# A two-layer kernel: how its first batch is prepared, and when GpSimd does its odd jobs

## The chip, the cores and the metric

The kernel runs on one core of a Trainium2 chip. The metric is device time in microseconds (us) of one execution. TensorE is called PE here, VectorE DVE, ScalarE ACT, GpSimd POOL, and SyncE, which issues most of the DMAs, SP. Everything is float32. A difference of 0.2% (8.3 us) is about what can be told from no change at all.

## The reference, cut to what matters

The input x is 4 batches of 2048 rows of 256. Two layers are computed; each adds an attention-like part and a second part, both fed by the layer norm of its input.

```python
xn = layernorm(x)
r = sigmoid(xn @ Wa + ba);  i = sigmoid(xn @ Wx + bx)          # gates
at = sigmoid(Lam) * exp(-r * log 8);  bt = sqrt(1 - at*at) * (i * xn)
y = scan over time: y_t = at_t * y_{t-1} + bt_t                 # recurrence
# 4 of 16 heads per batch, chosen by top_k(softmax(mean_t(xn @ Wr + br)))
x = x + y + attention(xn, the 4 chosen heads) @ Wo + bo         # layer 0
xn = layernorm(x)
a = causal attention(xn, 16 heads of 16) @ W_o + b_o            # layer 1
xr, xk = mixes of xn with xn one row earlier (mu_r, mu_k)
x = x + a + sigmoid(xr @ W_r.T) * (relu(xk @ W_k.T)**2 @ W_v.T)
```

## The kernel before

The program is unrolled over the batches. Inside `in_order` the compute engines (PE, ACT, DVE, POOL) keep the order in which the code is written; SP is free of that, and so is the setup ahead of it, whose instructions are placed among the others when the program is built. Several streams of work are Python generators, advanced a step at a time by `steps`, so that their instructions interleave.

**Setup.** `load_x(0)` is called once for `x_next`, which nothing reads, and again in `prepared(0, ...)`: eight loads of 512 KB on SP. ACT issues the weights `wa`, `wx`, then the bias vectors into `rows` and `rowb` (15 small loads, L181 and L186), `wr`, `wo2`, and layer 1's weights. PE turns `rows` and `rowb` into columns (L189, L190), DVE copies them to `cols` (L191), and ACT makes `a_c` of them (L201, L202). The biases of the gates come from `cols` too. Then layer 1's value bias goes through `wo1` into `bo1_b` (L219 to L223), and `W_r`, `W_k`, `W_v` are turned (L231, L232).

**Norm of the first batch.** `go` in `prepared`: statistics of 16 tiles of 128 rows (L261, L262), one inverse root for all on POOL (L267), then for each of four blocks of 512 rows four normalised tiles (L274) and two turns into `xT` (PE L280, DVE L281). All of it runs ahead of the recurrence in batch 0; in later batches it runs under layer 1 of the batch before.

**Recurrence and choice.** `recurrence` computes 16 gate units (PE L296, four instructions each; ACT L298), then `chain` for each half of the channels: Exp, Square and Sqrt on ACT, products (L306, L314) and two scans (L318) on DVE. `choose` sums `xT` (L351), picks the heads (L359 to L379), loads their weights (L391 to L393) and scales them (L423 to L425). After the 16 steps come `added` (L432), queries (L462), keys (L479) and half of the values (`values0`, L448; its copies out of the banks, L450, alternate between ACT and DVE). Each of these ten steps also advances the recurrence by one.

**Attention 0.** `attention0` works on pairs of row tiles. It names its PSUM banks by hand: scores of the first tile go to banks 0, 5, 4, 7 and of the second to 2, 1, 3, 6. `lend(...)` makes the next users of `own_bank` take the banks named. In the first pair, values borrow banks 1 and 3, later 4 and 7.

**Layer 1.** Four groups `g` of four heads; in each, four blocks `q` of 512 rows; in each, `4q + 4` units `t`. A group has 40 units. `Weights.scores` makes transposed scores (L828), exponentials (L830), and for the last four units of a block a mask on POOL (L833). `weigh`, one unit behind, multiplies by the values (L839); ACT copies the product out (L845) and POOL adds it up (L846). `Leading` runs the row maxima (L803, L806, L809) 20 units ahead, and SP writes them into row 16 of each head's strip in the query tile (L873). POOL also does these jobs: for `0 < g < 3` it clears the next group's two strips (`heads.open`, L741) in units 0 and 2 of block 1, and `heads.copy` (L747) sends eight copies through SP from unit 3; in odd groups it multiplies a block by its inverse sums (L922) 12 slots after the block ended, two slots per unit (`spread` comes by DMA L918 and is shuffled on DVE, L921); and in group 1 it adds `bo1_b` to one tile of x in each of the first 16 units (L958).

Of the kernel before, what the change touches and what calls it, by code (L numbers as in the profile page):

```python
# [10 lines left out]
FP = mybir.dt.float32  # L11
# [7 lines left out]
P = 128  # L19
# [57 lines left out]
def two_layers(ctx: ExitStack, tc: tile.TileContext, x, Wa, Wx, ba, bx, Lam,  # L77
# [61 lines left out]
        n0 = n % (NT // 2)  # L139
        return both[n // (NT // 2)][:, n0:n0 + count, :]  # L140

    x_next = load_x(0)


    ident = const.tile([P, P], FP, tag="ident", name="ident")
# [26 lines left out]
        ACT.dma_start(t, v.partition_broadcast(P))  # L172
        return t

    wa, wx = load_w(Wa, "wa"), load_w(Wx, "wx")


    rows = c4.tile([18, P], FP, tag="c4", name="rows")
    POOL.memset(rows, 0.0)
    for i, v in enumerate((ba, bx, Lam, mu_r, mu_k, bo, bv1, bq1, bk1)):  # L180
        ACT.dma_start(rows[2 * i:2 * i + 2, :], v.rearrange("(c p) -> c p", p=P))  # L181

    rowb = c4.tile([3 * NH, P], FP, tag="c4", name="rowb")
    for i, v in enumerate((bq, bk, bv)):
# [26 lines left out]
    for i in range(2):  # L211
        ACT.dma_start(wo2[i * DH:(i + 1) * DH, :, :], Wo.rearrange("(k d) e -> d k e", d=DH))

    wq1, wk1 = load_w(Wq1, "wq1"), load_w(Wk1, "wk1")
    wv1 = load_w(Wv1, "wv1")
    wo1, bo1_b = load_w(Wo1, "wo1"), load_row(bo1, "bo1_b")

    bv_b = c4.tile([P, 2, P], FP, tag="c4", name="bv_b")
    DVE.tensor_copy(bv_b, bv1_c.unsqueeze(2).to_broadcast([P, 2, P]))  # L219
    ps = bank()  # L220
    for c in range(2):
        PE.matmul(ps[:, 0:D], lhsT=bv_b[:, c, :], rhs=wo1[:, c, :], start=(c == 0), stop=(c == 1))
    DVE.tensor_tensor(bo1_b, ps[:, 0:D], bo1_b, ALU.add)  # L223

    def transposed(w, name):
        n = load_w(w, name + "_n", c4, "c4")
        t = const.tile([P, 2, D], FP, tag=name, name=name)
        ps = bank().rearrange("p (c d) -> p c d", c=2)
        for c in range(2):
            for d in range(2):  # L230
                PE.transpose(ps[:, c, d * P:(d + 1) * P], n[:, d, c * P:(c + 1) * P], ident)  # L231
        DVE.tensor_copy(t, ps)  # L232
        return t

    w_rT, w_kT, w_vT = transposed(W_r, "w_rT"), transposed(W_k, "w_kT"), transposed(W_v, "w_vT")

    DVE.tensor_scalar(w_vT, w_vT, 0.5, None, ALU.mult)


    nms = []  # L240
# [200 lines left out]
    def values0(b, xT, wv_, v, banks_of):  # L441

        for n in range(NT // 2):
            ps = banks_of[0]()
            for i in range(2):
                t = 2 * n + i
                for c in range(2):
                    PE.matmul(ps[:, i * D:(i + 1) * D], lhsT=xT[c][:, t * P:(t + 1) * P], rhs=wv_[:, c, :],  # L448
                              start=(c == 0), stop=(c == 1))
            (DVE.tensor_copy if n % 2 else ACT.copy)(rows_of(v, 2 * n, 2), ps.rearrange("p (n d) -> p n d", d=D))  # L450
            yield

    def queries0(b, k, xT, ch, bank):
# [120 lines left out]
    def attention0(b, xT, xt, ch, recurring, first, v, rest_of_values, norm, opening, leading):  # L574
# [20 lines left out]
        for n in range(NA * NP):  # L595
# [38 lines left out]
            if before:  # L634
                for j, i, to in ((0, 0, 1), (0, 1, 3), (1, 0, 6)):
                    late.turn(j, i, *of(to))
                    late.keep(j, i, ACT.copy)
            else:
                lend(1, 3)
                steps(rest_of_values, 2)  # L640
                lend()
            for j, i in ((0, 0), (1, 1), (1, 0), (0, 1)):
# [241 lines left out]
    def layer1(b, heads, vs, opening, x1, prepare, leading):  # L884
# [15 lines left out]
        def divide(g, q, o):  # L900


            i, blk = g % 2, slice(q * QB, (q + 1) * QB)
            part = vals[g // 2][:, blk]

            if i == 0:
                sums[q] = sm.tile([P, QB // 16], FP, tag=f"sums1_{q}", name=f"sums1_{b}_{g}_{q}", bufs=1)
            few = sums[q]
            SP.dma_start(few[64 * i:64 * i + 64, :], o[DH1:P:32, :].rearrange("h (a r) -> h a r", a=16))
            for h in range(4):  # L910
                row = (4 * i + h) * DH1
                SP.dma_start(part[row:row + DH1, :], o[32 * h:32 * h + DH1, :])
            if i == 0:
                return

            def invert():
                DVE.reciprocal(few, few)
                SP.dma_start(spread[0:P:16, :].rearrange("h (a r) -> h a r", a=16), few)  # L918

            def multiply():  # L920
                DVE.stream_shuffle(spread, spread, [0] * 16 + [16] * 16)  # L921
                POOL.tensor_tensor(part, part, spread, ALU.mult)  # L922
                if g == NG - 1:
                    mixing.append(mix.block(q))
            later.put(8, invert)
            later.put(12, multiply)

        def weigh(before):
            g, q, unit = before
# [6 lines left out]
            steps(opening, 1)  # L936
        before = None
        for n, (g, q, w) in enumerate(attending()):
            if q == 1 and 0 < g < NG - 1:
                if w.t in (0, 2):  # L940
                    heads.open(g + 1, w.t // 2)
                elif w.t == 3:
                    heads.copy(g + 1, slice(0, T))
            m = leading.next()
            for h in range(0, 4, 2):
                w.scores(h)
                w.scores(h + 1)
                if m is not None:
                    m.scores(2 - h)
                    m.scores(3 - h)  # L950
            if before is not None:
                weigh(before)
            later.slot()
            later.slot()
            before = (g, q, w)
            if g == 1 and n % 40 < NT:
                xs = rows_of(x1, n % 40, 1)[:, 0, :]
                POOL.tensor_tensor(xs, xs, bo1_b, ALU.add)  # L958
            if g == NG - 1 and q == 2:
                steps(mix.ahead, 1)  # L960

            for _ in range(2 if m is None else 0):
                if mixing and not steps(mixing[0], 1):
                    mixing.pop(0)
            if g == NG - 1:
                if q == 0 and w.first:
                    norming, choosing = prepare()
                elif m is None:
                    steps(norming, 2)
# [75 lines left out]

    def prepared(b, ready):

        xt = load_x(b)
        norm = Norm(xt, f"0_{b}", own_bank)
        ch = Chosen()  # L1050
        ready.append((xt, norm.xT, ch))

        def go():
            for t in range(0, NT, 2):
                norm.stats(t)
                norm.stats(t + 1)
                yield
            norm.inverse(0, NT)
            yield
            for q in range(NQ):  # L1060
                norm.rows(q, 0, 2)
                yield
                norm.rows(q, 2, 4)
                yield
                yield
                for c in range(2):
                    norm.turn(q, c, DVE.tensor_copy)
                    yield
        return go(), choose(b, norm.xT, ch)

    NOTHING = iter(()), iter(())

    with in_order(tc):
# [2 lines left out]
        mixing = iter(())  # L1076
        for b in range(B):
            xt, xT, ch = ready.pop()
            steps(norming, 100)
            recurring = recurrence(b, xT, xt, ch)  # L1080
            for _ in range(16):
                steps(recurring, 1)
                steps(mixing, 2)
                steps(choosing, 1)
            steps(mixing, 100)
            steps(choosing, 100)
            v = [half_tile(f"v0_{b}_{i}").rearrange("p (n f) -> p n f", f=NA * DH) for i in range(2)]
# [4 lines left out]
            for stream, count in ((querying, 4), (keying, 2), (valuing, 4)):  # L1092
                for _ in range(count):
                    steps(stream, 1)
                    steps(recurring, 1)

            banks_of[0] = bank
            x1, norm = xt, Norm(xt, f"1_{b}", bank)
# [37 lines left out]
```

## Time and profile before

| | us |
|---|---|
| median of 3 runs (lowest to highest) | 4131.89 (4131.09 to 4131.98) |
| the profiled execution's own time | 4131.89 |
| its span | 4130.2 |
| PE busy | 4059.9 (98%) |
| DVE busy | 2937.5 (71%) |
| ACT busy | 2892.1 (70%) |
| POOL busy | 1058.9 (26%) |

The span is what the trace covers; 1.7 us of the execution lie around it. PE's share is so high that the time is almost the sum of its work and its stops, so the table of who waited for whom on PE is the list of what can be had without less work on PE. A page's busy share counts modelled matmul ends, and cannot show a PE at half its clock; the granted clock does.

### The profile page before, as it was taken

Reading aid. Unit: us, or ns where it says so; the run is one execution under the profiler, and the core shown is the slowest. Engines: PE = TensorE matmul, PEld = TensorE weight load, DVE = VectorE, ACT = ScalarE, POOL = GpSimd, SP = SyncE. Lnnn points to the kernel's source line nnn. Section 1 sums busy time; section 2 is a strip of 40 time slices with the busy share of each in tenths; the row PEclk is TensorE's granted clock in tenths of the full one; section 3 lists DMA queues with packets and bytes.
Section 4 is the critical chain, followed back from the end, with each engine's and each line's share of the span. In section 5 each row is a group of like instructions: output and inputs, shape, how many; then the busy total and the mean of one; then the engine's idle time right before and its main releaser. Section 6 shows DMA issues by size and latency. Waiting matters only on the chain.

```text
span 4130.2 us, 86165 instructions
## 1 busy us (share of the span) xinstructions
PE 4059.9 (98%) x32994; PEld 2275.4 (55%) x32994; DVE 2937.5 (71%) x7036; ACT 2892.1 (70%) x6593; POOL 1058.9 (26%) x1334
## 2 busy tenths in 40 slices
PE   6999999999999999999999999999999999999998
PEld 3777743335577774333457776433446777643334
DVE  5656778887566668888656566888856656688882
ACT  3777658886677766888667775688756777578874
POOL 0000016544100002654410000365450000036544
PEclk9999999999999999999999999999999999999999
DMA  3000011100100001110010000101000000101000
GB/s 89 1 12 2 7 19 18 37 7 17 28 2 12 1 9 17 18 38 7 18 25 1 12 1 12 16 16 38 7 19 24 1 12 1 22 6 18 18 6 24
DMA packets 70816, 65.77 MB, mean 16 GB/s; under 512 B 37234, under 2 KB 58628, under 8 KB 68868
## 3 DMA queue, kind: packets, MB, share of 16 engines
q1 hardware_dynamic: 66624, 57.19, 6.5%
q8 instruction: 260, 4.26, 0.4%
q10 hardware_dynamic: 3780, 3.07, 0.3%
q14 instruction: 152, 1.25, 0.1%
HBM read 16.70 MB, written 8.39 MB: 6 GB/s over the span
## 4 chain that ended last, share of the span: by engine, by line
PE 94%; DVE 3%; ACT 1%; POOL 1%; DMA 1%; issue 0%; ACTq 0%; SPq 0%; POOLq 0%; DVEq 0%
PE bank L828 15%; PE bank L803 13%; PE bank L839 13%; PE bank L521 11%; PE bank L546 11%; PE bank L500 11%; PE bank L1024 4%; PE bank L730 3%; PE bank L296 3%; PE bank L559 2%; PE bank L762 1%; PE bank L462 1%; PE bank L1012 1%; PE bank L479 1%; DVE mx L809 1%; PE bank L280 1%
## 5 line engine op out<-in xcount | busy, mean ns | idle before, releaser
L830 ACT ACTIVATE p<-bank 128x512 f32<-128x512 f32 (+3 forms) x2560 | 1175.2, 539 | 291.3 <-PE bank L828 156.2
L803 PE MATMUL bank<-k,q 32*128 32x512 f32 (+3 forms) x5120 | 1138.5, 566 | 4.4 <-DVE mx L809 1.3
L809 DVE TENSOR_REDUCE mx<-bank 128x1 f32<-128x512 f32 x1536 | 953.1, 683 | 216.2 <-PE bank L803 216.0
L828 PE MATMUL bank<-q,k 32*128 32x512 f32 (+3 forms) x5120 | 1091.6, 556 | 0.0
L846 POOL TENSOR_TENSOR o<-o,w 128x512 f32<-128x512 f32 (+3 forms) x576 | 628.0, 1090 | 760.0 <-ACT w L845 748.3
L515 ACT ACTIVATE p<-bank,nm 128x512 f32<-128x512 f32 x1024 | 696.6, 700 | 58.5 <-DVE nm L508 58.1
L828 PEld LDWEIGHTS bank<-q,k 32*128 32x128 f32 x5120 | 420.7, 184 | 532.8 <-ACT p L830 446.7
L504 DVE TENSOR_REDUCE mx<-bank 128x1 f32<-128x512 f32 x1024 | 635.4, 683 | 86.6 <-PE bank L500 86.6
L527 ACT COPY pT<-bank 128x512 f32<-128x512 f32 x768 | 404.7, 598 | 306.4 <-PE bank L521 303.9
L839 PE MATMUL bank<-p,v 128*17 128x512 f32 (+3 forms) x5120 | 602.7, 534 | 16.4 <-POOL p L833 11.5
L521 PEld LDWEIGHTS bank<-ident,p 128*128 128x128 f32 x4096 | 446.1, 141 | 143.3 <-issue 116.6
L806 DVE CUSTOM_DVE_ANT_0 bank<-bank,cmask 128x512 f32<-128x512 f32 (+3 forms) x1024 | 473.4, 521 | 70.8 <-PE bank L803 51.0
L521 PE MATMUL bank<-ident,p 128*128 128x128 f32 x4096 | 508.5, 276 | 0.0
L803 PEld LDWEIGHTS bank<-k,q 32*128 32x128 f32 x5120 | 430.2, 183 | 133.7 <-DVE mx L809 36.6
L267 POOL TENSOR_TENSOR rs<-rs,minus_half 128x4 f32<-128x4 f32 (+1 forms) x20 | 27.9, 1395 | 1852.1 <-DVE rs L266 1828.1
L546 PEld LDWEIGHTS bank<-pT,v 128*64 128x64 f32 x8192 | 444.5, 137 | 95.3 <-ACT p L515 94.0
L500 PE MATMUL bank<-k,q 64*128 64x512 f32 x2048 | 496.4, 603 | 0.0
L546 PE MATMUL bank<-pT,v 128*64 128x128 f32 x8192 | 475.4, 274 | 0.0
L845 ACT COPY w<-bank 128x512 f32<-128x512 f32 (+3 forms) x576 | 304.4, 529 | 101.5 <-PE bank L839 76.0
L527 DVE COPY pT<-bank 128x512 f32<-128x512 f32 x256 | 164.8, 685 | 293.1 <-PE bank L521 291.8
L839 PEld LDWEIGHTS bank<-p,v 128*17 128x17 f32 x5120 | 89.7, 95 | 431.5 <-ACT p L830 236.4
L833 POOL TENSOR_SCALAR_AFFINE_SELECT p<-p 128x256 f32<-128x256 f32 x512 | 206.8, 416 | 313.4 <-ACT p L830 306.8
(164 smaller groups left out, 3323.1 us busy)
## 6 DMA issues: line engine op xcount, KB each, us to landing
x<-in_L_attn_x_dram SPq DMA_DIRECT2D x20, 512.0 KB
q<-q SPq DMA_DIRECT2D x64, 128.0 KB
vals<-o SPq DMA_DIRECT2D x256, 32.0 KB
out_dram<-x SPq DMA_DIRECT2D x32, 256.0 KB
q<-qp SPq DMA_DIRECT2D x48, 128.0 KB
k<-kp SPq DMA_DIRECT2D x48, 128.0 KB
q<-nmT SPq DMA_DIRECT2D x256, 2.0 KB
q<-qp SPq DMA_DIRECT2D x64, 32.0 KB
```

The lines of the kernel that those rows point to most:

```text
L500: PE.matmul(self.s[j][i], lhsT=self.qT[i][half_, self.t * P:(self.t + 1) * P], rhs=self.kT[half_, j * QB:(j + 1) * QB], start=True, stop=True)
L504: DVE.tensor_reduce(self.mx[:, n:n + 1], self.s[j][i], AX.X, ALU.max)
L515: ACT.activation(self.p[j][:, i, :], self.s[j][i], AF.Exp, bias=self.nm, accum_out=self.sums[:, n:n + 1])
L521: PE.transpose(to[:, n * P:(n + 1) * P], self.p[j][:, i, n * P:(n + 1) * P], ident)
L527: copy(self.pT[:, n0:n0 + 4, :], self.tr[j, i].rearrange("p (n q) -> p n q", q=P))
L546: PE.matmul(acc[i * DH:(i + 1) * DH, 0:P], lhsT=self.v[h][:, n, self.k * DH:(self.k + 1) * DH], rhs=tile_.pT[:, 8 * h + n, :], start=(n == ...
L803: PE.matmul(s[:, 0:n], lhsT=self.qT[strip(h), self.qs], rhs=self.kT[strip(h), self.ks], start=True, stop=True)
L809: DVE.tensor_reduce(self.mx[:, h, :], s[:, 0:n], AX.X, ALU.max)
L828: PE.matmul(s[:, c0:QB], lhsT=self.kT[strip(h), self.ks], rhs=self.qT[strip(h), self.q0 + c0:self.q0 + QB], start=True, stop=True)
L830: ACT.activation(p[:, h % 2, c0:QB], s[:, c0:QB], AF.Exp, scale=SC1)
L839: PE.matmul(acc[32 * h:32 * h + DH1 + 1, c0:QB], lhsT=self.v[h], rhs=self.p[h // 2][:, h % 2, c0:QB], start=True, stop=True)
L846: POOL.tensor_tensor(self.o[:, c0:QB], self.o[:, c0:QB], w[:, c0:QB], ALU.add)
```

## The change

- x of batch 0 is loaded once: `x_first`, which `prepared` uses.
- The vectors stand ahead of `wa`, `wx` in the code. Layer 1's weights and `bo1_b` are loaded through SP, behind x. The three that are turned go into one `half` tile, `w_n`. Their preparation (a DVE copy, four matmul instructions, one add, twelve transposes, three copies, one scaling) moves behind batch 0's first values, into the fixed order.
- Batch 0's norm goes by blocks: statistics, inverse, rows and turns of a block are one step. Two blocks come before the recurrence; blocks 2 and 3 follow its gate units 0 and 1. The choice begins two units later.
- `values0` copies on ACT except for its second pair. In the first pair of `attention0` the two banks lent are the two of 1, 2, 3, 6 that have been longest out of use.
- In layer 1 the strips are cleared in units 0 and 2 of block 2 (copies from unit 3); the multiply of block 0 comes 16 slots after instead of 12; `bo1_b` is added in units 0 to 7 of blocks 2 and 3.

```diff
-    x_next = load_x(0)
+    x_first = load_x(0)
...
-    wa, wx = load_w(Wa, "wa"), load_w(Wx, "wx")
-
     rows = c4.tile([18, P], FP, tag="c4", name="rows")
     POOL.memset(rows, 0.0)
     for i, v in enumerate((ba, bx, Lam, mu_r, mu_k, bo, bv1, bq1, bk1)):
         ACT.dma_start(rows[2 * i:2 * i + 2, :], v.rearrange("(c p) -> c p", p=P))
+    wa, wx = load_w(Wa, "wa"), load_w(Wx, "wx")
...
+    def load_late(w, t):
+        SP.dma_start(t, w.rearrange("(c p) f -> p c f", p=P))
         return t
 
-    w_rT, w_kT, w_vT = transposed(W_r, "w_rT"), transposed(W_k, "w_kT"), transposed(W_v, "w_vT")
-
-    DVE.tensor_scalar(w_vT, w_vT, 0.5, None, ALU.mult)
+    wq1, wk1, wv1, wo1 = (load_late(w, const.tile([P, 2, D], FP, tag=n, name=n))
+                          for n, w in (("wq1", Wq1), ("wk1", Wk1), ("wv1", Wv1), ("wo1", Wo1)))
+    bo1_b = const.tile([P, D], FP, tag="bo1_b", name="bo1_b")
+    SP.dma_start(bo1_b, bo1.partition_broadcast(P))
+    as_given = half_tile("w_n")[:, 0:6 * D].rearrange("p (w c d) -> p w c d", w=3, c=2)
+    w_rn, w_kn, w_vn = (load_late(w, as_given[:, i]) for i, w in enumerate((W_r, W_k, W_v)))
...
-            (DVE.tensor_copy if n % 2 else ACT.copy)(rows_of(v, 2 * n, 2), ps.rearrange("p (n d) -> p n d", d=D))
+            (DVE.tensor_copy if n == 1 else ACT.copy)(rows_of(v, 2 * n, 2), ps.rearrange("p (n d) -> p n d", d=D))
...
-                lend(1, 3)
+                lend(*sorted((1, 2, 3, 6), key=lambda i: (i - turn[0] - 1) % 8)[:2])
...
-            later.put(12, multiply)
+            later.put(12 if q else 16, multiply)
...
-            if q == 1 and 0 < g < NG - 1:
+            if q == 2 and 0 < g < NG - 1:
                 if w.t in (0, 2):
                     heads.open(g + 1, w.t // 2)
...
-            if g == 1 and n % 40 < NT:
-                xs = rows_of(x1, n % 40, 1)[:, 0, :]
+            if g == 1 and q >= 2 and w.t < 8:
+                xs = rows_of(x1, 8 * (q - 2) + w.t, 1)[:, 0, :]
                 POOL.tensor_tensor(xs, xs, bo1_b, ALU.add)
...
+        def go_by_blocks():
+            for q in range(NQ):
+                for t in range(4 * q, 4 * q + 4):
+                    norm.stats(t)
+                norm.inverse(4 * q, 4)
+                norm.rows(q, 0, 4)
+                for c in range(2):
+                    norm.turn(q, c, DVE.tensor_copy)
+                yield
...
-            steps(norming, 100)
+            steps(norming, 100 if b else 2)
             recurring = recurrence(b, xT, xt, ch)
-            for _ in range(16):
+            for n in range(16):
                 steps(recurring, 1)
+                steps(norming, 1)
                 steps(mixing, 2)
-                steps(choosing, 1)
+                if b or n >= 2:
+                    steps(choosing, 1)
...
+            if b == 0:
+                bv_b = c4.tile([P, 2, P], FP, tag="c4", name="bv_b")
+                DVE.tensor_copy(bv_b, bv1_c.unsqueeze(2).to_broadcast([P, 2, P]))
+                ps = bank()
+                for c in range(2):
+                    PE.matmul(ps[:, 0:D], lhsT=bv_b[:, c, :], rhs=wo1[:, c, :], start=(c == 0), stop=(c == 1))
+                DVE.tensor_tensor(bo1_b, ps[:, 0:D], bo1_b, ALU.add)
...
+                w_rT, w_kT, w_vT = transposed(w_rn, "w_rT"), transposed(w_kn, "w_kT"), transposed(w_vn, "w_vT")
+                DVE.tensor_scalar(w_vT, w_vT, 0.5, None, ALU.mult)
```

More of the change, by code (lines that the diff above doesn't have):

```diff
@@ L212, in two_layers @@
         ACT.dma_start(wo2[i * DH:(i + 1) * DH, :, :], Wo.rearrange("(k d) e -> d k e", d=DH))
[L214 to L232, printed above, removed]
-        return t
-    w_rT, w_kT, w_vT = transposed(W_r, "w_rT"), transposed(W_k, "w_kT"), transposed(W_v, "w_vT")
-    DVE.tensor_scalar(w_vT, w_vT, 0.5, None, ALU.mult)
+    def load_late(w, t):
+        SP.dma_start(t, w.rearrange("(c p) f -> p c f", p=P))
+        return t
+    wq1, wk1, wv1, wo1 = (load_late(w, const.tile([P, 2, D], FP, tag=n, name=n))
[4 more added lines that the diff above has]
+    w_rn, w_kn, w_vn = (load_late(w, as_given[:, i]) for i, w in enumerate((W_r, W_k, W_v)))
     nms = []
@@ L1046, in prepared @@
     def prepared(b, ready):
-        xt = load_x(b)
+        xt = load_x(b) if b else x_first
         norm = Norm(xt, f"0_{b}", own_bank)
@@ L1068, in go @@
                     yield
-        return go(), choose(b, norm.xT, ch)
+        return go() if b else go_by_blocks(), choose(b, norm.xT, ch)
     NOTHING = iter(()), iter(())
@@ L1095, in two_layers, with transposed @@
                     steps(recurring, 1)
+            if b == 0:
[5 more added lines that the diff above has]
+                DVE.tensor_tensor(bo1_b, ps[:, 0:D], bo1_b, ALU.add)
+                def transposed(w, name):
+                    n = w
+                    t = const.tile([P, 2, D], FP, tag=name, name=name)
+                    ps = bank().rearrange("p (c d) -> p c d", c=2)
+                    for c in range(2):
+                        for d in range(2):
+                            PE.transpose(ps[:, c, d * P:(d + 1) * P], n[:, d, c * P:(c + 1) * P], ident)
+                    DVE.tensor_copy(t, ps)
+                    return t
+                w_rT, w_kT, w_vT = transposed(w_rn, "w_rT"), transposed(w_kn, "w_kT"), transposed(w_vn, "w_vT")
+                DVE.tensor_scalar(w_vT, w_vT, 0.5, None, ALU.mult)
             banks_of[0] = bank
```

## The prediction

> **What bounds the kernel now.** I read the table of waits on PE first, since PE is busy for 98% of the span, then the places of its longest rows. The columns are: who waited for what, us in total, times, longest.
>
> ```profile
> PE bank L189 <- DVE mv L262: 22.4, 1, 22.4
> PE bank L839 <- POOL p L833: 11.5, 20, 1.0
> PE bank L448 <- DVE v L450: 6.1, 4, 1.5
> ...
> PE bank L190 <- DMA rowb<-in_L_ffn_bv_dram: 3.2, 1, 3.2
> ```
>
> The first and last rows are the start. The second is POOL's masks (2.9 us a batch), the third a stop in each batch where layer 0's attention begins. The timeline of the start (start us, us, engine, line):
>
> ```profile
> 11.56 0.51 ACTq L181 DMA_DIRECT2D rows<-in_L_attn_ba_dram  x1
> 17.94 0.43 DVE L261 BATCH_NORM_STATS2 st<-x 128x6 f32<-128x256 f32 x1 [12.56 <-DMA x<-in_L_attn_x_dram]
> 25.88 0.31 PE L190 MATMUL bank<-ident,rowb 48*128 48x48 f32 x1 [3.20 <-DMA rowb<-in_L_ffn_bv_dram]
> 39.28 1.37 DVE L274 TENSOR_SCALAR xn<-x,mv,rs 128x256 f32<-128x256 f32 x4
> 42.68 1.37 DVE L274 TENSOR_SCALAR xn<-x,mv,rs 128x256 f32<-128x256 f32 x4
> 45.23 8.89 PE L296 MATMUL bank<-xT,wa 128*128 128x512 f32 x16
> ```
>
> Statistics cannot begin before 17.94, as the x that is used is loaded behind one that nobody reads. The vectors land at 25.9. A block of norm takes DVE 3.4 us from rows to rows (39.28 to 42.68). The gates start at 45; they end at 75.1, where L432 begins. What follows is where the weights' preparation will go:
>
> ```profile
> 87.61 7.17 PE L448 MATMUL bank<-wv,xT 128*128 128x256 f32 x32
> 94.72 1.99 PE L500 MATMUL bank<-k,q 64*128 64x512 f32 x8
> 98.23 3.72 PE L448 MATMUL bank<-wv,xT 128*128 128x256 f32 x16 [1.53 <-DVE v L450]
> ```
> ```profile
> 95.24 2.35 DVE L318 TENSOR_TENSOR_SCAN y<-at,y,bt 128x1024 f32<-128x1024 f32 x1
> 97.51 0.67 DVE L450 COPY v<-bank 128x512 f32<-128x512 f32 x1
> 98.09 1.28 DVE L332 TENSOR_SCALAR y<-y,added 128x2048 f32<-128x2048 f32 x1
> ```
>
> DVE is in its scans until 97.5 and does L332 next, in program order. In layer 1, group 1, POOL (first three lines) keeps PE (last) waiting:
>
> ```profile
> 711.12 1.26 POOL L922 TENSOR_TENSOR vals<-vals,spread 128x512 f32<-128x512 f32 x1
> 712.35 0.72 POOL L958 TENSOR_TENSOR x<-x,bo_b 128x256 f32<-128x256 f32 x1
> 713.03 0.76 POOL L833 TENSOR_SCALAR_AFFINE_SELECT p<-p 128x256 f32<-128x256 f32 x2
> ```
> ```profile
> 713.48 0.97 PE L839 MATMUL bank<-p,v 128*17 128x256 f32 x8 [1.03 <-POOL p L833]
> ```
>
> **The start.** The dead load goes: 2.1 MB at the 243 GB/s of the window from 0 to 25 us. x's first block shares the engines with `wa`: 0.79 MB at 243 GB/s is 3.2 us; a lone 0.26 MB load takes 2.75 us in the chain (`wo`, issued at 24.61), 1.67 more than its bytes. So it lands at 0.81 + 1.67 + 3.2 = 5.7. A block then costs DVE 2.1 (four statistics pairs of 0.53: 17.94 to 26.41 for sixteen), 0.2 (L266), 1.0 (POOL's power on 128x4, L267), 0.3 for the two hand-overs (26.70 to 26.86 is one) and 3.4: 7.0 us. Four blocks: `xT` is whole at 5.7 + 28 = 33.7, against 46.2 (45.47 + 0.69), if nothing holds DVE; x arrives faster than one block in 7 us.
>
> The vectors may hold it. `cols` (L191) is in DVE's queue too, among the blocks. In the code the vectors already stood ahead of `wr`, `wo2` and layer 1's weights, yet these were issued from 1.91 to 10.16 and the vectors from 11.56: their place in the code did not decide, so moving them past `wa` need not help. What helps is fewer bytes: x 2.10, eleven weights of 0.262, `bo1_b` 0.13 make 5.1 MB, 21.1 us at 243 GB/s, so vectors that come among the last land near 22, and near 6 if truly first. Since they used to come behind nearly everything, I take 22. DVE reaches the rows' end of block 1 at 5.7 + 7 + 4.9 = 17.6; if `cols` stands there, it waits 4.4 and spends 0.4 on the small column operations: `xT` is whole at 38.5.
>
> Gate units 0 and 1 are then done beside the blocks; 14 units remain, from 0.8 before that. 14 x 1.72 (sixteen instructions in 7.03 at 61.26, four to a unit) is 24.1, L359 0.35, and 2.0 for the slow clock (the first sixteen took 8.89; granted clock 0.50 from 40 to 49). The gates end at 38.5 - 0.8 + 26.4 = 64.1 instead of 75.1: **-11.0**. Bounds: -15.8 (`xT` at 33.7); -2.5 if vectors at 26 hold three blocks (26 + 21 = 47). The choice starts two units later, but its scaled weights come about 23 us after `xT` (69.6 before, against 46.2), and queries need them 27.5 after: hidden by 4 us. ACT has 15 small issues and its table loads behind the vectors, ready about 4 us after them (25.59 to 29.90): ahead of the remaining gates. The late weights lie on SP behind x only; the next thing on SP is the choice's loads, 20 us later.
>
> **The weights' preparation.** Before, it lay among the start's stops. Now it stands in PE's and DVE's order. On the clock of before: PE has its fourth value pair done at 94.7; `bv_b` comes behind L332, which without the copy at 97.51 ends at 98.8: `bv_b` 99.1 (0.29). PE stops 4.4 us. Four instructions like L448's (3.72 / 16 = 0.23) and twelve transposes (L521: 2.35 / 20 = 0.12) take 2.3: 101.4. Scores 2.0, value pairs 4 and 5 3.5: 106.9; ACT's copy 0.6 and its table load 1.28 (100.86) put the first exponential at 108.8, against 102.16; PE's next values wait for the third exponential as now (0.47 at 104.33). So **+6.6**, the 1.53 us stop included. Queued behind PE's wait are the first pair's scores, and DVE's maxima and ACT's exponentials wait for them. Below: +2.3, if only PE's own work counted.
>
> PE falls to half its clock after one long stop of the profile:
>
> ```profile
> 4114.38 3.66 PE L1024 MATMUL bank<-w_vT,ka 128*128 128x256 f32 x8 [3.90 <-POOL ka L1014]
> 4119.60 1.89 PE L1024 MATMUL bank<-w_rT,xr 128*128 128x256 f32 x8
> ```
>
> The stop of 3.90 us makes eight products take 3.66 instead of 1.89: +1.8 us. A stop of 4.4 us would do that at most once: the bound above is +8.4. The Trainium skill's page "TensorE: Matmul & The Clock Gate" (Part 1) says why it is no certainty: the gate judges free-running windows of about 3.4 us, so the stop must cover one. By that rule a stop of 4.4 covers a window about 3 times in 10, and the sum would be 1.8 higher then; the trace agrees, as its 1.53 us stops leave the clock at 1.00 (75 to 100 us).
>
> **Value copies and lent banks, batches 1 to 3.** PE's stop at 98.23 is a bank whose copy stands behind the scans; it goes. But what is late next is ACT: pair 5 ends at 96.7 + 3.5 = 100.2, its copy, now ACT's, at 100.8, the table load at 102.1; the first exponential was at 102.16. The next values start 0.1 sooner. -0.1 x 3 = **-0.3**; bounds: -6.0 (all of 1.53 + 0.47 in three batches) and +0.9 (ACT's copy of pair 7 delays two turns by 0.3).
>
> **GpSimd's jobs.** Clearing (3.6 us), the adds (0.7 each) and the early multiply leave the masked units of block 1. The stops there are 1.03 (713.48, group 1) and 0.35 (933.78, group 3, the multiply of block 0) in each batch: 1.38 x 4 = **-5.5**. The waits at the batch's end (0.37, 0.10, 0.40, 0.71 from 1044) have other causes and stay. In block 2 a unit takes 2.9 us (723.98 to 726.96) and POOL has 1.27 + 0.73 of work, 3.8 with a strip to clear, caught up one unit later. The eight copies now stand among the sums of block 1 on SP: POOL is done clearing near 721, SP issues eight copies and five others by 728, and they land 12 us after the first (bytes of that batch run from 695.9 to 707.7), about 732; group 2's maxima need them at 739. Hidden by 7 us. `spread` of block 1 (727.13) queues behind the last copies, and DVE shuffles it at 732: 0 to 3 us a batch, taken as 0.
>
> **Sum.** -11.0 + 6.6 - 0.3 - 5.5 = -10.2. The profiled execution took 4131.89 (span 4130.2 and 1.7 around it), which is the median too: **4121.7**. 0.2%, 8.3 us, is about what a measurement of this kernel can tell from no change.
>
> **Rivals.**
> 1. *The vectors hold DVE longer* (26, before block 1): the start gains 2.5 instead of 11.0: 4130.2, no change. For it: ACT issued the vectors late before, and SP now puts 2 MB into the same engines. Against: fewer bytes in all. 0.16.
> 2. *The vectors are early*, DVE never waits: -15.8 for -11.0: 4116.9. For it: with layer 1's weights off its queue, ACT has nothing else to issue. 0.11.
> 3. *Slower: the strips' copies come behind SP's wait.* At 727.87 SP, with the sums of block 1 issued, has only the row maxima of block 3 left (L873, issued at 739.05). If clearing ends later than that, or its copies are queued behind L873, they are issued from 741.4 and land at 753; PE, which needs the strips at 739, stops 14 us, in groups 1 and 2 of four batches: +112, 4233.7. Against: POOL has 7 us to spare. 0.10.
>
> **How the numbers follow.** The forecast has 0.63, of which the half clock after the stop (4123.5) is a part. Its own range is 4114 to 4128: 0.46 faster by over 8.3 us (below 4123.6), 0.16 within, 0.01 slower. With rival 2: faster 0.57. With rival 1: same 0.32. Rival 3: slower 0.11. The range runs from 4111 (rival 2 with the values' full gain) to 4132 (rival 1 with the half clock) and leaves out rival 3.
>
> **What would show it.** The first statistics start near 6, the first gate before 25, L432 near 64; a stop on L222 of about 4 us, released by `bv_b`; L448 still waiting for ACT's exponentials; no wait of L839 for masks in block 1 of groups 1 and 3. I am wrong in the start if `cols` waits elsewhere, and in layer 1 if L803 waits for a DMA or DVE waits for `spread`.

## The result, and the profile after

| kernel | median | lowest to highest | runs |
|---|---|---|---|
| before | 4132.1 us | 4130.3 to 4133.4 | 20 |
| after | 4126.0 us | 4124.0 to 4129.9 | 20 |

The ratio is 0.9988 (95% interval 0.9982 to 0.9993): 6.1 us faster, where 4121.7 was forecast, and less than the 8.3 us (0.2%) that the forecast took as its bound for a change. The profiled execution of the kernel after took 4129.4 (span 4127.5), at the slow end of its runs. So its trace shows more of the cost than the median does; the 2.7 us by which its span is shorter are the sum to be explained first.

The changed program's lines are some 13 smaller: L296 is L282 now, L432 L418, L448 and L450 L434 and L437, L500 L487, L515 L502, L274 and L281 L260 and L267, L191 L190, L803 L790, L833 L820, L839 L826. L222 and its `bv_b` are L1103 and L1100.

The table of waits on PE (who waited for what, us in total, times, longest):

```profile
PE bank L188 <- DMA rowb<-in_L_ffn_bk_dram: 9.3, 1, 9.3
PE bank L434 <- ACT p L502: 8.7, 4, 2.2
PE bank L826 <- POOL p L820: 6.2, 12, 0.7
PE bank L1103 <- DVE bv_b L1100: 4.3, 1, 4.3
```

The 22.4 us of the start are gone. A wait of 9.3 us for the vectors is left on PE; what it costs is the time in which it holds DVE, shown next. The masks went from 11.5 to 6.2. New are 2.2 us in every batch before the last value pairs, where 1.53 + 0.47 stood, and the stop on `bv_b`. DVE's timeline of the start (start us, us, engine, line):

```profile
5.64 0.43 DVE L247 BATCH_NORM_STATS2 st<-x 128x6 f32<-128x256 f32 x1 [0.26 <-DMA x<-in_L_attn_x_dram]
16.24 1.38 DVE L260 TENSOR_SCALAR xn<-x,mv,rs 128x256 f32<-128x256 f32 x4 [1.13 <-POOL rs L253]
22.69 0.69 DVE L267 COPY xT<-bank 128x512 f32<-128x512 f32 x1 [5.07 <-PE bank L266]
27.17 0.23 DVE L190 COPY cols<-bank 128x66 f32<-128x66 f32 x1 [1.85 <-PE bank L189]
29.80 1.38 DVE L260 TENSOR_SCALAR xn<-x,mv,rs 128x256 f32<-128x256 f32 x4 [1.12 <-POOL rs L253]
36.83 1.38 DVE L260 TENSOR_SCALAR xn<-x,mv,rs 128x256 f32<-128x256 f32 x4 [1.12 <-POOL rs L253]
39.63 0.69 DVE L267 COPY xT<-bank 128x512 f32<-128x512 f32 x1 [0.16 <-PE bank L266]
```

x lands at 5.6, a block takes 7.0 us (29.80 to 36.83), and twice DVE is held in the second and third block, by 5.07 and 1.85, each time through a transpose of vectors in PE's queue. `xT` is whole at 40.3 (46.2 before). PE's timeline where layer 0's attention begins, batch 0, then batch 1:

```profile
88.59 2.05 PE L1103 MATMUL bank<-wo,bv_b 128*128 128x256 f32 x4 [4.34 <-DVE bv_b L1100]
90.43 2.14 PE L1112 MATMUL bank<-ident,w_n 128*128 128x128 f32 x12
92.92 2.06 PE L487 MATMUL bank<-k,q 64*128 64x512 f32 x8 [0.35 <-DVE w_kT L1113]
102.73 3.50 PE L434 MATMUL bank<-wv,xT 128*128 128x256 f32 x15 [2.19 <-ACT p L502]
...
1111.29 3.72 PE L434 MATMUL bank<-wv,xT 128*128 128x256 f32 x16
1114.94 1.99 PE L487 MATMUL bank<-k,q 64*128 64x512 f32 x8
1119.11 5.41 PE L434 MATMUL bank<-wv,xT 128*128 128x256 f32 x16 [2.19 <-ACT p L502]
```

The same sixteen products take 3.72 us before the stop and 5.41 after it. The table by stretches says why (the column behind the engines' busy times is the granted TensorE clock):

```profile
core 0: us, PE busy (x) PEld busy (x) DVE busy (x) ACT busy (x) POOL busy (x), PEclk, DMA share, GB/s
1115.80:1119.20 3.40, 1.22 (x7) 0.35 (x5) 2.81 (x7) 3.39 (x8) 0.00 (x0) 1.00 0.00 0
1119.20:1122.60 3.40, 3.40 (x8) 2.68 (x9) 0.00 (x0) 3.20 (x10) 0.00 (x0) 0.50 0.00 0
1122.60:1126.00 3.40, 3.40 (x25) 3.12 (x24) 0.94 (x2) 1.31 (x3) 0.00 (x0) 1.00 0.00 0
```

For 3.4 us after the stop PE has half its clock; such a stretch is called a window below, and one costs half its length, 1.7 us. This happens in batches 1, 2 and 3 and after the stop on `bv_b`, and in none of these places before. The kernel's last stop, of 3.90 us in both, is followed by a window before and by a stretch of two (6.8 us) after:

```profile
4110.41 3.92 PE L1012 MATMUL bank<-w_vT,ka 128*128 128x256 f32 x8 [3.90 <-POOL ka L1002]
4114.12 2.87 PE L1012 MATMUL bank<-wo,vals 128*128 128x256 f32 x8
```

These groups took 3.66 and 1.89 before, so the end is 1.2 us slower.

Where the time went is read by landmarks, the same instruction's start after minus before:

| landmark | before | after | difference | of this stretch |
|---|---|---|---|---|
| first of `added` (L432), batch 0 | 75.09 | 64.56 | -10.5 | start -10.5 |
| first projection (L559) | 122.31 | 120.71 | -1.6 | preparation +8.9 |
| first gate of batch 1 | 1051.38 | 1047.84 | -3.5 | layer 1 -1.9 |
| first projection, batch 1 | 1140.54 | 1138.78 | -1.8 | value pairs +1.8 |
| first gate of batch 2 | 2070.63 | 2067.10 | -3.5 | layer 1 -1.8 |
| end | 4130.2 | 4127.5 | -2.7 | two batches: values +3.6, layer 1 and end -2.7 |

Start -10.5, preparation +8.9, value pairs +5.3, layer 1 and the end -6.4: -2.7. The last batch gives only -1.2 of the -6.4, as the slower end of 1.2 us is in it.

### The profile page after: what moved, and what is told of

It is laid out like the page before. It is cut to its first block, busy times and chain, and to the rows that moved or that the text cites. A ratio compares the mean times of both kernels' runs of the same rounds, so it can differ in the third digit from the quotient of the medians.

```text
span 4127.5 us, 86156 instructions
## 1 busy us (share of the span) xinstructions
PE 4063.5 (98%) x32994; PEld 2281.0 (55%) x32994; DVE 2931.8 (71%) x7027; ACT 2897.4 (70%) x6605; POOL 1059.6 (26%) x1337
## 4 chain that ended last, share of the span: by engine, by line
PE 95%; DVE 2%; ACT 1%; POOL 1%; DMA 0%; issue 0%; SPq 0%; ACTq 0%; POOLq 0%; DVEq 0%
PE bank L815 16%; PE bank L790 13%; PE bank L826 13%; PE bank L508 11%; PE bank L533 11%; PE bank L487 11%; PE bank L1012 4%; PE bank L717 3%; PE bank L282 3%; PE bank L546 2%; PE bank L749 1%; PE bank L449 1%; PE bank L434 1%; PE bank L466 1%; PE bank L1000 1%; DVE mx L796 1%
## 5 line engine op out<-in xcount | busy, mean ns | idle before, releaser
L790 PE MATMUL bank<-k,q 32*128 32x512 f32 (+3 forms) x5120 | 1139.8, 566 | 4.5 <-DVE mx L796 1.3
L833 POOL TENSOR_TENSOR o<-o,w 128x512 f32<-128x512 f32 (+3 forms) x576 | 627.7, 1090 | 746.6 <-ACT w L832 739.4
L502 ACT ACTIVATE p<-bank,nm 128x512 f32<-128x512 f32 x1024 | 695.5, 699 | 56.0 <-DVE nm L495 55.8
L826 PE MATMUL bank<-p,v 128*17 128x512 f32 (+3 forms) x5120 | 599.6, 534 | 11.4 <-POOL p L820 6.2
L790 PEld LDWEIGHTS bank<-k,q 32*128 32x128 f32 x5120 | 430.8, 183 | 133.9 <-DVE mx L796 36.4
L487 PE MATMUL bank<-k,q 64*128 64x512 f32 x2048 | 496.3, 603 | 0.3 <-DVE w_kT L1113 0.3
L826 PEld LDWEIGHTS bank<-p,v 128*17 128x17 f32 x5120 | 88.9, 95 | 423.8 <-ACT p L817 237.1
L820 POOL TENSOR_SCALAR_AFFINE_SELECT p<-p 128x256 f32<-128x256 f32 x512 | 205.9, 413 | 319.6 <-ACT p L817 313.1
```

What stands on the lines that cost most here:

```text
L487: PE.matmul(self.s[j][i], lhsT=self.qT[i][half_, self.t * P:(self.t + 1) * P], rhs=self.kT[half_, j * QB:(j + 1) * QB], start=True, stop=True)
L502: ACT.activation(self.p[j][:, i, :], self.s[j][i], AF.Exp, bias=self.nm, accum_out=self.sums[:, n:n + 1])
L790: PE.matmul(s[:, 0:n], lhsT=self.qT[strip(h), self.qs], rhs=self.kT[strip(h), self.ks], start=True, stop=True)
L826: PE.matmul(acc[32 * h:32 * h + DH1 + 1, c0:QB], lhsT=self.v[h], rhs=self.p[h // 2][:, h % 2, c0:QB], start=True, stop=True)
L833: POOL.tensor_tensor(self.o[:, c0:QB], self.o[:, c0:QB], w[:, c0:QB], ALU.add)
```

## The experiments

Each kernel was compared with the kernel before on one chip, whose medians there were 4131.7 to 4131.9. The differences below are to the 4126.0 of the kernel after, beside which the kernel before had 4132.1; a few tenths of a us may come of that.

**GpSimd's jobs alone.** The kernel before, with:

```
-            later.put(12, multiply)
+            later.put(12 if q else 16, multiply)
-            if q == 1 and 0 < g < NG - 1:
+            if q == 2 and 0 < g < NG - 1:
-            if g == 1 and n % 40 < NT:
-                xs = rows_of(x1, n % 40, 1)[:, 0, :]
+            if g == 1 and q >= 2 and w.t < 8:
+                xs = rows_of(x1, 8 * (q - 2) + w.t, 1)[:, 0, :]
```

> The kernel before, with the moves of GpSimd's work alone: strips cleared and copied in block 2 instead of 1, bo1 added in blocks 2 and 3, the first block's product 4 slots later. Theory A (they take away one stop of 1.03 us and one of 0.35 in each batch, which shift PE's work by 1.77 us between the two profiled executions): 4132.1 - 7.1 = 4125.0, and the runs lie as close together as those of the kernel before. Theory B (only the stops as listed): 4132.1 - 5.5 = 4126.6. If other parts of the change do the work in layer 1: no change.

Measured: 4124.0 (4120.8 to 4126.0), ratio 0.9981 (0.9972 to 0.9990), -7.9 us. This part alone gains more than the whole change; the rest of the change gives 2 us back on the median (ten of these eleven runs lie below the 4126.0 of the kernel after, though the two intervals overlap). That the runs would lie as close as before's was a miss. Layer 1's masked products before (933.78, group 3) and after (930.60):

```profile
933.78 0.97 PE L839 MATMUL bank<-p,v 128*17 128x256 f32 x8 [0.35 <-POOL p L833]
```
```profile
930.60 0.63 PE L826 MATMUL bank<-p,v 128*17 128x256 f32 x8
```

The listed stop of 0.35 is not all: the eight products last 0.97 instead of 0.63, since the second half waits again, for the second of POOL's two selects. At 713.48 it was 0.97 too, and 0.63 at that place now. So the two places cost 1.03 + 0.35 + 2 x 0.34 = 2.1 us a batch, not 1.38; the landmarks of the kernel after give 1.8 to 1.9 in the first two batches.

**Value copies and lent banks back.** The kernel after, with the copies and `lend` of before:

```
-            (DVE.tensor_copy if n == 1 else ACT.copy)(rows_of(v, 2 * n, 2), ...)
+            (DVE.tensor_copy if n % 2 else ACT.copy)(rows_of(v, 2 * n, 2), ...)
-                lend(*sorted((1, 2, 3, 6), key=lambda i: (i - turn[0] - 1) % 8)[:2])
+                lend(1, 3)
```

> The kernel after, with the value copies (DVE for every odd pair) and the two lent banks as before the change. Theory A (the one long stop of 2.19 us in batches 1 to 3, which took the place of 1.53 + 0.47, calls the half clock, 3.41 us at half speed, 1.7 us each): the two short stops come back, no half-clock window follows them in batches 1 to 3, each of these batches gets 1.8 us shorter than in the profiled execution of the kernel after; the median falls from 4126.0 to between 4121 and 4124, and the runs lie closer together than 4124.0 to 4129.9. Theory B (the windows come by where the kernel stands in time, whatever the stop): windows of half clock stay near these places, and the median changes by 0.2 x 3 = 0.6 us at most.

Measured: 4123.0 (4120.4 to 4125.6), ratio 0.9978 (0.9969 to 0.9987), 3 us below the kernel after; ten of the eleven runs lie no higher than the fastest of the kernel after. The range is 5.3 us wide, against 5.8, so hardly narrower. Batch 1, PE:

```profile
1111.09 3.72 PE L434 MATMUL bank<-wv,xT 128*128 128x256 f32 x16 [1.53 <-DVE v L437]
1117.23 3.07 PE L434 MATMUL bank<-wv,xT 128*128 128x256 f32 x13 [0.45 <-ACT p L502]
```

The two short stops are back, the products take 3.72, and no window of half clock follows in batches 1 to 3. This part of the change is a loss; Theory A holds, but for the spread.

**A shorter stop, with the change's copies and banks.** In the first pair of a batch ACT takes the lent banks' exponentials first:

```
-            for j, i in ((0, 0), (1, 1), (1, 0), (0, 1)):
+            for j, i in ((0, 0), (1, 1), (1, 0), (0, 1)) if before else ((1, 1), (1, 0), (0, 0), (0, 1)):
-            lend(4, 7)
+            lend(*((4, 7) if before else (7, 4)))
```

> The kernel after, with its copies and lent banks kept; in the first pair of each batch alone, ACT takes the exponentials of the two lent banks (7, then 4) first, and the last value pairs take the banks in that order. So the stop is released by the first exponential instead of the third, two exponentials of 0.7 us sooner: 2.19 becomes about 0.8 us in all four batches. Theory A (the length of the stop calls the half clock): no half-clock window at these places, the time falls by 1.4 x 4 for the stops and by 1.7 for each window that a run of the kernel after has, to about 4118. Theory B (the windows come by place in time): windows stay, 4126.0 - 5.6 = 4120.4 at best. Theory C (what is late next takes it back: the first transposes wait for the same exponentials): no change.

Measured: 4119.3 (4118.0 to 4122.8), ratio 0.9971 (0.9960 to 0.9982), 6.7 us below the kernel after.

```profile
1117.51 3.72 PE L434 MATMUL bank<-wv,xT 128*128 128x256 f32 x16 [0.85 <-ACT p L502]
1121.07 2.35 PE L508 MATMUL bank<-ident,p 128*128 128x128 f32 x20
```

0.85 us in all four batches, and no window after any. Nothing later takes it back.

**A middle and a longer stop.** One kernel has only the second of the two edits above. In the other the lent banks' exponentials come last, and `lend(4, 7)` stays:

```
+            ... if before else ((0, 0), (0, 1), (1, 1), (1, 0)):
```

> The kernel after; in the first pair of each batch alone, the last value pairs take the lent banks in the order 7, 4, so that the stop is released by the second exponential instead of the third: 2.19 becomes about 1.5 us. Theory A (as for the longer stop): no window at these four places, the time falls by 0.67 x 4 = 2.7 and by the two windows of 1.7 that a run of the kernel after has on the mean, to about 4120. Theory B (windows by place in time, or by chance whatever the stop): some of the four stops are followed by windows, and the time falls by 2.7 to 4123.3.

> The kernel after; in the first pair of each batch alone, ACT takes the exponentials of the lent banks (7 and 4) last, so that the stop before the last value pairs is released by the fourth exponential instead of the third: 2.19 becomes about 2.85 us in all four batches. Theory A (windows of half clock start on a grid of 3.41 us that runs free of the kernel, and one is called when at least 2.0 us of the grid window before lie in the stop; 1.9 or less call none): a stop of 2.85 meets this for 2.3 of 3.4 us of its possible places, so about three of the four stops are followed by a window, each exactly where 2.0 or more overlap; the time rises by 0.66 x 4 = 2.6 and by 0.2 x 4 x 1.7 = 1.3 for the windows, to about 4130. Theory B (only a window that is idle throughout calls the half clock): none of the four. Theory C (a later wait takes the longer stop back): no change.

Measured, middle: the stop is 1.52 in all four batches, with no window; 4121.7 (4118.9 to 4124.2), ratio 0.9975 (0.9965 to 0.9985), between the two times expected. Longer: the stop is 2.85, the median 4128.3 (4121.9 to 4134.6), ratio 0.9989 (0.9980 to 0.9998). Of the four stops in its profiled execution none is followed by a window, where I expected three. The rule held: windows of this trace fall at 86.78 plus multiples of 3.413, so the stop from 1115.99 to 1118.84 lies 1.62 in one and 1.23 in the next, and the other three have 1.46, 1.79 and 1.58 at most. My count of three was wrong, as the four are not independent: the batches took 1017.0 to 1017.4 us there, 297.95 to 298.06 windows, so all four stops stand at nearly one place of the grid, all hit or all spared. Theory B predicted the same none; the windows after stops of 2.19 us, which are shorter than a window (3.41 us), decide against it. The other executions left no trace, but their mean granted clocks are on record: five of 4121.9 to 4124.7 us have 0.998, five of 4128.3 to 4130.5 have 0.996, and the one of 4134.6 has 0.993. Groups like these are what all hit or all spared would give; stretches in layer 1, described at the end, lower the same mean, so it is not shown. Since the runs spread so widely, no change of the median against the kernel after is shown either. By stretches, batch 1:

```profile
1114.19:1117.60 3.41, 1.80 (x8) 0.49 (x6) 3.29 (x7) 3.38 (x7) 0.00 (x0) 1.00 0.00 0
1117.61:1121.00 3.39, 2.16 (x10) 1.93 (x11) 0.19 (x2) 3.39 (x11) 0.00 (x0) 1.00 0.00 0
```

**New banks with the old copies.** The kernel after, with the copies of before (the first of the two lines changed in the experiment that puts both back) and the change's lent banks:

> The kernel after, with the copies as before the change (DVE for every odd pair) and the new choice of lent banks. Theory A (ACT is late next: the copy of pair 5, now ACT's, stands ahead of the first exponential): ACT is 0.6 us sooner, the stop before the last value pairs is about 1.6 us instead of 2.19, and there is none of 1.53 before pair 4. Theory B (the first exponential waits for DVE's scans and maxima): 2.19 us as in the kernel after.

Measured: 4121.1 us in a single execution, which weighs little; the trace says more.

```profile
1115.90 1.13 PE L487 MATMUL bank<-k,q 64*128 64x512 f32 x4 [1.31 <-DVE v L437]
1117.34 4.97 PE L434 MATMUL bank<-wv,xT 128*128 128x256 f32 x14 [0.31 <-ACT p L502]
```

Neither theory: the stop before pair 4 went, but the scores of the second tile now wait 1.31 for DVE's copy, and the last pairs 0.31 for ACT. With less of the copying, ACT is sooner, as Theory A said, and DVE is late. One of its three such places (batch 1) was followed by half clock; the last section returns to it.

**The preparation among the gates.** The block `if b == 0:` moved, unchanged, into the loop of the gate units:

```
                 if b or n >= 2:
                     steps(choosing, 1)
+                if b == 0 and n == 8:
+                    bv_b = c4.tile([P, 2, P], FP, tag="c4", name="bv_b")
+                    ...
```

> The kernel after, with the preparation of layer 1's weights moved from after the fourth value pair to after the ninth gate unit of the first batch. Theory A (the preparation costs 8.9 us in the profiled execution because PE waits for bv_b behind the scans on DVE, 4.34 us, with a half-clock window of 1.7 us, and then stops 2.2 us for ACT's exponentials): among the gates DVE is free, only PE's own 2.3 us are left, the time falls by 5 to 6.6 us, to about 4120. Theory B (the stop only moves: the first scores then wait for DVE's scans all the same, and the stop before the last value pairs grows by what was saved): the time falls by 0 to 2 us.

Measured: 4118.4 (4115.5 to 4119.5, five runs), ratio 0.9966 (0.9952 to 0.9979), 7.5 us below the kernel after.

```profile
52.55 1.10 PE L1090 MATMUL bank<-wo,bv_b 128*128 128x256 f32 x4 [0.19 <-DVE bv_b L1087]
53.49 1.47 PE L1099 MATMUL bank<-ident,w_n 128*128 128x128 f32 x12
54.80 5.32 PE L282 MATMUL bank<-xT,wa 128*128 128x512 f32 x12
...
96.28 3.72 PE L434 MATMUL bank<-wv,xT 128*128 128x256 f32 x16 [2.19 <-ACT p L502]
```

The gates start again 2.25 us after 52.55, L418 starts 2.35 later than in the kernel after (66.91), and the stop before the last pairs is still 2.19. So Theory A: where DVE is free, the preparation costs what PE works.

**The vectors first.** The kernel after, with the fifteen loads ahead of `x_first = load_x(0)`, kept in order, and without `POOL.memset(rows, 0.0)`:

```
+    with in_order(tc):
+        rows = c4.tile([18, P], FP, tag="c4", name="rows")
+        for i, v in enumerate((ba, bx, Lam, mu_r, mu_k, bo, bv1, bq1, bk1)):
+            ACT.dma_start(rows[2 * i:2 * i + 2, :], v.rearrange("(c p) -> c p", p=P))
+        rowb = ...
     x_first = load_x(0)
```

> The kernel after, with the fifteen loads of the vectors put first on ACT's queue, ahead of x in the program, and without the clearing of rows, which all nine vectors overwrite. Theory A (the vectors are late because each of their loads waits for an earlier load to complete, and DVE is held 5.07 + 1.85 us by them): rows and rowb land before 12 us, blocks 1 to 3 follow one another in 7 us each, xT is whole near 34 instead of 40.3, and the time falls by 6 to 7 us, to about 4119.5. Theory B (small loads are slow in themselves, or wa, now behind them, becomes late): the first gate moves later, x's blocks come late, and the time changes by less than 3 us or rises.

Measured: 4123.4 (4121.0 to 4125.4), ratio 0.9979 (0.9970 to 0.9988), 2.6 us below the kernel after: neither 6 to 7 nor nothing. ACT's first issues after the change, and two of DVE's rows in the experiment:

```profile
9.01 0.35 ACTq L185 DMA_DIRECT2D rowb<-in_L_ffn_bq_dram  x1
11.88 0.48 ACTq L179 DMA_DIRECT2D rows<-in_L_attn_ba_dram  x1
```
```profile
12.16 0.23 DVE L191 COPY cols<-bank 128x66 f32<-128x66 f32 x1 [1.90 <-PE bank L190]
20.61 0.17 DVE L203 TENSOR_SCALAR a_c<-a_c 128x2 f32<-128x2 f32 x1 [1.77 <-ACT a_c L202]
```

The vectors are issued from 0.81 to 8.8 and `cols` is copied at 12.2 instead of 27.2. But DVE still waits 1.90 for `rowb`, and 1.77 for ACT, which stands behind the issue of `wo2` (`wo` in the trace). Of the 6.92 us of the two holds, 3.25 are won, and the first of `added` starts 3.2 us sooner (61.35). In the compiled program eight semaphores (the counters by which a load reports that it has landed) serve all loads. From the ninth on, an issue waits until an earlier load has landed, and everything behind it on that queue waits too: in the kernel after, ACT issues the second half of `wo2` at 5.37 us, when `wa`, which had the same semaphore, has landed at 5.35. So the vectors were late in their issue, for the loads that had to land before them.

**The start, with that mended.** The kernel after; ACT issues only the nine vectors of `rows`, `wa` and `wx`, ahead of x in the program and without the clearing of `rows`, as in the run before. All the rest goes behind x on SP, and `rowb` is turned later (only this last part is shown):

```
-    PE.transpose(pv[:, 18:18 + 3 * NH], rowb, ident[:3 * NH, :3 * NH])
-    DVE.tensor_copy(cols, pv[:, 0:18 + 3 * NH])
+    DVE.tensor_copy(cols[:, 0:18], pv[:, 0:18])
...
+                if b == 0 and n == 2:
+                    pb = bank()
+                    PE.transpose(pb[:, 0:3 * NH], rowb, ident[:3 * NH, :3 * NH])
+                    DVE.tensor_copy(cols[:, 18:18 + 3 * NH], pb[:, 0:3 * NH])
```

> The kernel after, with the nine vectors of rows and then wa and wx as ACT's only loads, everything else that is not x behind x on SP's queue, and the head biases (rowb) turned and copied apart, at the third gate unit. Theory A (what held DVE in the run with the vectors first was rowb, 1.90 us, and the Ln of Lam on ACT behind the issue of wo, 1.77 us, not the start itself): the four blocks follow one another in 7 us, xT is whole near 33.5 instead of 40.3 us, L418 starts near 58 instead of 64.6, and the time is 6 to 6.8 us below the kernel after: about 4119.5. Theory B (x or the gate weights become late, or the choice is late for the queries by as much as the start gains): the gain stays below 3.5 us.

Measured: `xT` is whole at 33.6 us, L418 (L420 here) starts at 57.51, 7.05 before the kernel after.

```profile
16.60 1.38 DVE L262 TENSOR_SCALAR xn<-x,mv,rs 128x256 f32<-128x256 f32 x4 [1.13 <-POOL rs L255]
23.55 1.38 DVE L262 TENSOR_SCALAR xn<-x,mv,rs 128x256 f32<-128x256 f32 x4 [1.12 <-POOL rs L255]
30.50 1.38 DVE L262 TENSOR_SCALAR xn<-x,mv,rs 128x256 f32<-128x256 f32 x4 [1.12 <-POOL rs L255]
32.31 1.29 DVE L269 COPY xT<-bank 128x512 f32<-128x512 f32 x2 [0.42 <-PE bank L268]
```

The time is 4121.3 (4119.8 to 4123.3), ratio 0.9976 (0.9966 to 0.9986), 4.6 us below the kernel after, not 6 to 6.8. At the first projection 5.8 of the 7.05 are left, as batch 0's stop of 2.19 is followed by half clock here (95.21) and not in the kernel after. The start's gain itself is not given back: the profiled executions, each with three windows after its four stops of 2.19, differ by 6.8 us in their spans (4120.7 against 4127.5). That the medians differ by only 4.6 may be the clock in other executions; no run shows it.

**All three edits together** (the start, the preparation among the gates, the shorter stop):

> The kernel after with three edits at once: the loads of the start as in e7, the preparation of the weights among the gates as in e2, and the first pair's order of exponentials as in e5. If the three terms are independent (6.5 from the start, 7.5 from the preparation, 5.6 and about two windows of 1.7 from the stops, of which batch 0's stop counts in each): 4126.0 - 6.5 - 7.5 - 7 = 4105, give or take 4. If they share a bound (the scans on DVE, or the choice's weights, which come some 23 us after xT): the start's gain is given back at the first queries or the first exponential, and the time is 4110 to 4114.

Measured: 4108.8 (4106.7 to 4110.7, five runs), ratio 0.9943 (0.9930 to 0.9957): 23 us faster than before and 17 faster than after. The terms nearly add: alone they gave 4.6, 7.5 and 6.7 us, 18.8 together, and at once 17.2. The waits on PE that are left:

```profile
PE bank L268 <- DVE xn L262: 11.6, 7, 4.7
PE bank L828 <- POOL p L822: 5.9, 12, 0.7
PE bank L1014 <- POOL ka L1004: 3.9, 1, 3.9
PE bank L436 <- ACT p L504: 3.4, 4, 0.8
```

## Why the prediction was right or wrong

**The start: right.** -11.0 was forecast and -10.5 measured: x at 5.6 (5.7), 7.0 us a block, `xT` whole at 40.3 (38.5), L432 at 64.56 (64.1). The hold was 6.9 instead of 4.4 us, in two places. That their place in the code did not decide was right; the reason, bytes ahead of them, was not the whole of it: each issue waits for an earlier load. With that mended, rival 2's `xT` of 33.7 came (33.6). Rival 1 did not occur.

**The preparation: mechanism right, size wrong.** +6.6 was forecast, with a bound of +8.4; it was +8.9. The stop (4.34, forecast 4.4) and PE's work (2.25, forecast 2.3) were right. The sum lacked the wait for `w_kT` (0.35) and the longer stop before the last pairs. Above all the half clock came: four products and twelve transposes took 2.05 and 2.14 instead of 1.10 and 1.47. I gave it 3 chances in 10. That came from the rule of the Trainium skill's page "TensorE: Matmul & The Clock Gate" (Part 1), by which a stop must cover a window. In eight traces with this stop (4.3 to 4.9 us) the half clock followed in eight, and in four of them for two windows (6.83 us), so "at most once" was wrong too.

**Value pairs: the step that failed.** -0.3 was forecast, with bounds of -6.0 and +0.9; it was +5.3 in the profiled execution. That ACT is late next was right, and so was its price: without half clock, the way from the first scores to the first projection is 27.72 us (batch 1 of the kernel with the preparation among the gates) against 27.64 before. The failed step is that the half clock was put at nothing here: stops of 1.53 us that left the clock alone were taken as evidence for a new one. Two short stops merged into one of 2.19, and with a window behind it the same way takes 29.41 (batch 1 of the kernel after). Neither the sum nor its bounds contained that.

**GpSimd's jobs: too small.** -5.5 was forecast, -6.4 (profiled, with the slower end of 1.2 us in it) and -7.9 (alone, on the median) measured: the term counted the listed stops and left out the second wait inside the eight products. Rival 3 did not occur. SP issued the strips' copies 11 us ahead of the row maxima:

```profile
721.78 3.19 SPq L734 DMA_DIRECT2D k<-kp  x4
725.07 0.67 SPq L905 DMA_DIRECT2D spread<-sums  x1
736.49 2.31 SPq L860 DMA_DIRECT2D q<-nmT  x4
```

**The sum.** Without the four windows of 1.7 us the profiled execution would stand at -2.7 - 6.8 = -9.5, and without the slower end at -10.7, close to the -10.2 forecast. A gain in layer 1 larger than forecast offsets the longer hold and the wait for `w_kT`. The median, 3.4 us under the profiled execution, is what about two windows fewer would give; that the other executions had fewer is argued, since only one of them left a trace. Their mean granted clocks agree as far as three places go: 0.995 in the six of 4127.7 us and more, 0.996 in the fourteen below, though stretches in layer 1 count in these too. The range held the time, for reasons that it did not contain: its room up to 4132 came from rival 1, which did not occur, and not from windows behind the value pairs. The likelier outcome named, faster by over 8.3 us (0.57 with rival 2), did not come.

## What to carry to other kernels

In this kernel a stop of PE has two prices: its length, and 1.7 us more when it pulls the clock down; merging two short stops into one can cost more than both. Ask of every wait that is removed not only what is late next, but how long the stop then is in one piece, and whether the order of the work that releases it can shorten it. Count a stop over the whole group of instructions that it stretches, and put one-time work in PE's order where the engine that feeds it is free.

## What the runs showed of the hardware

**The half clock needs less than an idle window.** Its stretches begin on a grid of 3.413 us that lies elsewhere in each execution (in the kernel after 30.35 and 4109.27 are 1195 steps apart). Ten of the sixteen stops of 2.19 us in four kernels were followed by half clock; in each of the ten, 2.00 to 2.19 us lie in one step of the grid, in the other six 1.41 to 1.90 at most. (A step is one length of the grid, 3.413 us.) The kernel with the preparation among the gates has both: 1.90 and 2.19.

```profile
1108.62:1112.03 3.41, 1.51 (x8) 0.38 (x4) 3.20 (x7) 3.38 (x7) 0.00 (x0) 1.00 0.00 0
1112.04:1115.45 3.41, 3.13 (x15) 2.78 (x16) 0.00 (x0) 3.41 (x12) 0.00 (x0) 1.00 0.00 0
2125.80:2129.20 3.40, 1.21 (x6) 0.78 (x5) 2.17 (x5) 3.39 (x10) 0.00 (x0) 1.00 0.00 0
2129.21:2132.62 3.41, 3.41 (x10) 2.70 (x9) 0.00 (x0) 2.90 (x9) 0.00 (x0) 0.50 0.00 0
```

PE busy 1.51 us of the step kept the clock, 1.21 lost it. None of 15 stops of 1.52 or 1.53 and none of 8 of 0.85 was followed by one. The Trainium skill's page "TensorE: Matmul & The Clock Gate" (Part 1) gives the window as 3413 ns and free-running; the trace agrees. It puts the fall to half clock after an idle window of about 3.4 us; the trace differs: about 2.0 us of idle inside one window were enough here.

**Still open.** These figures hold for the place where they were read, and idle time alone does not decide. The kernel with new banks and old copies lost its clock in batch 1 with 1.62 us of stops in one step, and kept it in batch 2 with 1.62 too. Products of 64 rows stand there, so how many rows work may count, but no run tells that apart. At the start, where transposes fill part of a step, 1.32 us of stops were enough once (the step from 34.61 us with the shorter stop) and 1.29 were not (from 35.58 with the longer stop).

Layer 1 has stretches of half clock of 6.83 us, in none to four batches of an execution; each lengthens layer 1 by about 1.1 us. In the kernel before, the way from the first product of L803 to the end of the last of L839 is 546.34 us in batch 1, which has one, and 545.32 and 545.22 in batches 0 and 2, which have none. The same grid decides them. In each batch PE stops twice for about 0.33 us between products of 32 rows (L803, for DVE), 54.3 us apart. In the twelve traces, 23 of the 48 second stops began between 0.25 us before and 0.46 after the start of a step, and all 23 were followed by such a stretch; the other 25 began 1.31 to 3.12 us after one, and none was. None of the 48 first stops was. So one kernel's executions differ by where the grid lies, which widens the range of several kernels here. What in these products calls the half clock was not tested.
